# A four-layer graph network on one core: a new instruction plan for the pair distances, statistics by group, and layer 0 of the first groups ahead of the branch

## The chip, the core and the metric

The kernel runs on one core of a Trainium2 chip. A core has five engines that work through their own queues of instructions side by side: TensorE (PE, matrix products into PSUM), VectorE (DVE), ScalarE (ACT), GpSimd (POOL) and SyncE (SP, which here only issues transfers). They hand work to each other by semaphores; transfers between the large memory and the on-chip memory run on DMA engines. The metric is the time of one execution on the device in microseconds (us), from the first to the last instruction; the lower the better. Before the change it is 2890.65 us, the median of three runs (2886.53 to 2890.78).

## What is computed

128 graphs of 128 nodes with 128 features each (`x`), and their adjacency (`adj`, here zeros and ones), go through four residual layers. What matters here is cut from the reference:

```python
# layer 0
h = relu(layernorm(x))
for r in 1..7:                       # one relation per value of adj
    mask = (adj == r); degree = clip(mask.sum(axis=2), 1e-6)
    agg += (mask / degree @ h) @ rel_weights[r]
x = x + relu(layernorm(agg + h @ self_w.T + self_b) * gamma + beta)

# layer 1: attention from pairwise distances
h = relu(layernorm(x))
D = abs(h[:, :, None, :] - h[:, None, :, :])      # [128, 128, 128, 128]
p = D @ W1.T + b1                                 # 64 channels for each pair of nodes
p = (p - mean(p)) / sqrt(var(p) + eps) * g1 + be1 # statistics over all pairs of all graphs
A = softmax(where(adj > 0, leaky(p) @ W2.T + b2, -9e15))
y = A @ h @ Wg.T + bg;  y = leaky(batchnorm(y))   # statistics over all graphs
x = x + concat(h, y) @ Wt.T + bt
# layers 2 and 3: graph attention with 4 heads and with 1, each with its residual
```

Layer 1 needs the mean and the variance of `p` over all pairs of all graphs before any pair can be normalised. So the kernel has three stages: the first computes `p` for all graphs and writes it out, the second reads it back, and the third does layers 2 and 3.

## The kernel before

The graphs are handled in 32 groups of four (`G = 4`, `NG = 32`, `NB = 128`). A distance is symmetric, so only half of the pairs are computed, in four tiles per graph (`NT = 4`). Each tile passes through four engines:

```python
def difference(i):        # "d": tiles 0 and 2 on DVE, 1 and 3 on POOL
    eng = nc.gpsimd if on_pool else nc.vector
    eng.tensor_tensor(d, ahead, x[:, None, None, :].to_broadcast([P, 2, KC, P]),
                      OP.max if t == BY_MAX else OP.subtract)
def absolute(i):          # "abs": ACT; not for tile 0, which goes by the maximum
    nc.scalar.activation(diffs[i], diffs[i], AF.Abs)
def products(i):          # "hp": PE, 8 products for a tile, 16 for tile 0
    ... nc.tensor.matmul(hp[64 * hh:64 * hh + 64, c:c + 512], w1T2 if by_max else w1T, d[:, hh, c:c + 512], ...)
def evacuate(i):          # "hs": ACT copies PSUM out
    nc.scalar.copy(halves[b][:, t, :], linear.pop(i))
def statistics(i):        # "st": DVE
    nc.vector.bn_stats(st[:, 2 * t, :], hs[:, 0:512])
    nc.vector.bn_stats(st[:, 2 * t + 1, :], hs[:, 512:1024 - P * last])
    if last:
        nc.vector.bn_stats(st[:, 8, :], hs[:, 1024 - P:])
        nc.vector.bn_aggr(ST1[:, b, 0, :], st.rearrange("p a b -> p (a b)"))
        nc.vector.bn_aggr(ST1[:, b, 1, :], st[:, 8, :])
```

Beside the tiles, each group has the chain of layer 0 (`chain(g)`: load, two norms, degree, transposes, products, sum, and the norm `h1` that the distances start from) and two steps `features`, which transpose two graphs (`xp`), copy them (`xe`), double a part of the copy on POOL (`again`) and form a small product (`pw`, `xw`).

The order of instructions in the first stage isn't found by hand. Every step is declared with its engine, an assumed duration, the steps that it follows and a rank; a planner builds one list from them, engine by engine in time, and the kernel is emitted in that order. `HOP` is the assumed delay when work passes from one engine to another:

```python
PERIOD, FIRST, HOP, LANDING = 12.5, 4, 0.2, 3.0
def _ordered(steps, limits):
    def released(name):
        engine = named[name][1]
        ready[engine][name] = max([0.0] + [done[a] + HOP * (named[a][1] != engine) for a in waits[name]])
    ...     # the engine that can start first takes its ready step of lowest rank
...
step(("hs", i), "ACT", 0.9, [("hp", i), ("hs", i - 1)] + ..., i + 1, lambda: evacuate(i))
step(("st", i), "DVE", 1.8 if t == NT - 1 else 1.2, [("hs", i), ("st", i - 1)], i + 2, lambda: statistics(i))
```

Ahead of the first stage stands a prologue. The largest value in `adj` decides a branch: only if it is above 1 must relations 2 to 7 be computed. The whole of `adj` (8.4 MB) is scanned for it. In the order of the program: the inputs of the first two groups (`AHEAD = 2`) are asked for, `adj` is scanned in eight parts of 1 MB on DVE (four issued from ACT, four from SP, four buffers), layer 0 of the two groups runs up to its product, then the set-up for layers 2 and 3, then the branch, and behind it the rest of layer 0 of these groups:

```python
for c in range(8):
    part = sc.tile([P, n], I32, name="part", bufs=4)
    (nc.scalar if c < 4 else nc.sync).dma_start(part, flat[c])
    nc.vector.tensor_reduce(tops[:, c:c + 1], part, AX.X, OP.max)
...
for w in first:
    while next(w) != "rest":     # layer 0 of groups 0 and 1, up to the sum
        pass
nc.vector.tensor_scalar(flag, top, 1.5, None, op0=OP.is_gt)
...     # set-up for layers 2 and 3: transposes, small products, bounds, pieces in bf16
with tc.If(nc.values_load(flag, min_val=0, max_val=1) > 0) as cmp: ...   # relations 2 to 7
with cmp.Else():
    ...   # the sum starts from self_b
for _ in itertools.zip_longest(*first):
    pass                         # the rest of layer 0 of groups 0 and 1
```

Of the kernel before, what the change touches and what calls it, by code (L numbers as in the profile page):

```python
# [18 lines left out]
G = 4  # L19
# [13 lines left out]
AHEAD = 2  # L33
FETCHED = 10
# [5 lines left out]
PERIOD, FIRST, HOP, LANDING = 12.5, 4, 0.2, 3.0  # L40
TINY = 2.0 ** -100
# [71 lines left out]
def _ordered(steps, limits):  # L113
# [13 lines left out]
    def released(name):  # L127
        engine = named[name][1]
        ready[engine][name] = max([0.0] + [done[a] + HOP * (named[a][1] != engine) for a in waits[name]])
# [5 lines left out]
    while len(plan) < len(steps):  # L135
# [20 lines left out]
        for tag in gives:  # L156
            left[tag].append(start + cost + HOP)
# [9 lines left out]
def tile_gnn_stack(ctx: ExitStack, tc: tile.TileContext, a: dict, out: bass.AP):  # L167
# [47 lines left out]
    ST1 = res.tile([P, NB, 2, 2], F32, name="ST1")  # L215
# [41 lines left out]
    with tc.tile_pool(name="c0", bufs=1) as c0, tc.tile_pool(name="p0", bufs=2) as p0:  # L257

        both = c0.tile([P, 2, P], F32, name="both")
        nc.sync.dma_start(both[:, 0, :], a["rel_w"][1])  # L260
        nc.sync.dma_start(both[:, 1, :], a["self_wT"])
# [6 lines left out]

        AGG = [c0.tile([P, G, P], F32, name=f"agg{g}") for g in range(AHEAD)] + AGG
# [5 lines left out]

        def highest(sc):

            n = NB * P // 8
            tops = sc.tile([P, 8], F32, name="tops")
            flat = a["adj"].rearrange("b t s -> b (t s)").rearrange("b (c n) -> c b n", c=8)  # L280
            for c in range(8):
                part = sc.tile([P, n], I32, name="part", bufs=4)
                (nc.scalar if c < 4 else nc.sync).dma_start(part, flat[c])
                nc.vector.tensor_reduce(tops[:, c:c + 1], part, AX.X, OP.max)
            top = sc.tile([P, 1], F32, name="top")
            nc.vector.tensor_reduce(top, tops, AX.X, OP.max)
            pt = sm("ptop")
            nc.tensor.transpose(pt[0:1, 0, :], top, ident)
            nc.vector.tensor_reduce(top[0:1, :], pt[0:1, 0, :], AX.X, OP.max)
            return top[0:1, :]  # L290
# [8 lines left out]
        def act_norm(dst, src, rs, nb):  # L299

            for k in range(G):
                nc.scalar.activation(dst[:, k, :], src[:, k, :], AF.Relu, bias=nb[:, k:k + 1],
                                     scale=rs[:, k:k + 1])
# [4 lines left out]

        def layer0(g):
            bs = slice(g * G, g * G + G)  # L310
            x = p0.tile([P, G, P], F32, name="x")
            nc.sync.dma_start(x, a["x"][bs].rearrange("b t c -> t b c"))
            adj = p0.tile([P, G, P], I32, name="adj")
            nc.sync.dma_start(adj, a["adj"][bs].rearrange("b t s -> t b s"))
            yield
            mv = small.tile([P, G, 2], F32, name="lnmv")
            rs = small.tile([P, G], F32, name="lnrs")
            norm_stats(x, mv, rs)
            nb = shift(mv, rs)
            yield  # L320

            mask = p0.tile([P, G, P], F32, name="mask")
            nc.gpsimd.tensor_scalar(mask, adj, 1, None, op0=OP.is_equal)
            deg = small.tile([P, G], F32, name="deg")
            nc.vector.tensor_reduce(deg, mask, AX.X, OP.add)
            nc.vector.tensor_scalar(deg, deg, 1e-6, None, op0=OP.max)
            nc.vector.reciprocal(deg, deg)
            yield
            h = p0.tile([P, G, P], F32, name="hn")
            act_norm(h, x, rs, nb)  # L330
            nc.gpsimd.tensor_tensor(mask, mask, deg[:, :, None].to_broadcast([P, G, P]), OP.mult)
            nc.gpsimd.tensor_scalar(M8[g], adj, 0, None, op0=OP.is_gt)
            yield
            hT = p0.tile([P, G, P], F32, name="hT")
            transpose(hT, h)
            yield
            maskT = p0.tile([P, G, P], F32, name="maskT")
            transpose(maskT, mask)
            yield
            o = p0.tile([P, G, P], F32, name="o")  # L340
            hw = p0.tile([P, G, P], F32, name="hw")
            ph = sm("ph")
            for k in range(G):
                nc.tensor.matmul(ph[:, k, :], hT[:, k, :], both[:, 0, :], start=True, stop=True)
            nc.scalar.copy(hw, ph)
            yield
            po = sm("po")
            for k in range(G):
                nc.tensor.matmul(po[:, k, :], hT[:, k, :], both[:, 1, :], start=True, stop=False)
                nc.tensor.matmul(po[:, k, :], maskT[:, k, :], hw[:, k, :], start=False, stop=True)  # L350
            nc.vector.tensor_copy(o, po)
            yield "rest"
            nc.vector.tensor_tensor(o, o, AGG[g], OP.add)
            yield
            mv = small.tile([P, G, 2], F32, name="lnmv")
            rs = small.tile([P, G], F32, name="lnrs")
            norm_stats(o, mv, rs)
            yield
            for k in range(G):
                nc.vector.scalar_tensor_tensor(o[:, k, :], o[:, k, :], mv[:, k, 0:1], gamma,  # L360
                                               op0=OP.subtract, op1=OP.mult)
            yield
            on = sm("on")
            for k in range(G):
                nc.vector.scalar_tensor_tensor(on[:, k, :], o[:, k, :], rs[:, k:k + 1], beta,
                                               op0=OP.mult, op1=OP.add)
            nc.vector.scalar_tensor_tensor(x, on, 0.0, x, op0=OP.max, op1=OP.add)
            nc.sync.dma_start(X[g], x)
            yield
            norm_stats(x, MV1[:, g], RS1[:, g])  # L370
            nb = shift(MV1[:, g], RS1[:, g])
            yield
            H1[g] = p0.tile([P, G, P], F32, name="h1", bufs=3)
            act_norm(H1[g], x, RS1[:, g], nb)


        H1 = {}
        first = [layer0(g) for g in range(AHEAD)]
        for w in first:
            next(w)  # L380
        with tc.tile_pool(name="sc", bufs=1) as sc:
            top = highest(sc)
            flag = const.tile([1, 1], I32, name="flag")
            for t, v in ((gamma, "gamma"), (beta, "beta")):
                nc.vector.tensor_copy(t, load(v, [P, P], _bcast(a[v], P), pool=c0))
            for k in range(G):
                nc.sync.dma_start(selfb[:, k, :], _bcast(a["self_b"], P))
            for w in first:
                while next(w) != "rest":
                    pass  # L390
            nc.vector.tensor_scalar(flag, top, 1.5, None, op0=OP.is_gt)

        with tc.tile_pool(name="sw", bufs=1) as sw:


            w2x = const.tile([P, P + 8], F32, name="w2x")
            nc.sync.dma_start(w2x[:, 0:P], a["W_2"])
            w3x = const.tile([P, P + 2], F32, name="w3x")
            nc.sync.dma_start(w3x[:, 0:P], a["W_3"])
            b_2 = load("b_2", [P, P], _bcast(a["b_2"], P))  # L400
            b_2c = col("b_2c", a["b_2"])
            wtyT = load("wtyT", [P, P], a["WtT"][P:2 * P])
            a2 = const.tile([P, 2, 4], F32, name="a2")
            nc.vector.memset(a2, 0.0)
            a3 = const.tile([P, 2, 1], F32, name="a3")
            for part in range(2):
                for hd in range(4):

                    nc.sync.dma_start(a2[32 * hd:32 * hd + 32, part, hd:hd + 1], a["a_2"][32 * (1 - part):][0:32])
                nc.sync.dma_start(a3[:, part, :], a["a_3"][P * (1 - part):][0:P])  # L410
            add_b = sw.tile([P, 8], F32, name="add_b")
            bounds = sw.tile([P, 3, 8], F32, name="bounds")
            nc.vector.memset(bounds, 0.0)
            square = sw.tile([P, 10], F32, name="square")
            for wx, av, n in ((w2x, a2, 4), (w3x, a3, 1)):
                pt = sm("pwt")
                nc.tensor.transpose(pt[:, 0, :], wx[:, 0:P], ident)
                wt = sw.tile([P, P], F32, name=f"wt{n}")
                nc.scalar.copy(wt, pt[:, 0, :])
# [23 lines left out]
            nc.vector.tensor_copy(b_parts, part)  # L443
            ones3 = const.tile([3, P], BF16, name="ones3")
            nc.vector.memset(ones3, 1.0)
            nc.vector.tensor_tensor(bounds[:, 2, :], add_b, add_b, OP.mult)


            bound = sw.tile([P, 1], F32, name="bound")
# [1120 lines left out]
```

## Time and profile before

| | |
|---|---|
| time, median of three runs | 2890.65 us |
| span of the profiled execution | 2889.8 us, mean granted PE clock 0.952 |
| busy: PE, DVE, ACT, POOL | 2469.7, 2520.0, 2392.2, 1729.1 us |
| first distance on DVE starts | 81.24 us |
| first stage: first and last rows of `p` issued to memory | 102.98 and 1597.75 us |
| second stage: first and last rows read back | 1604.1 and 2346.5 us |
| last statistic of the second stage | 2410.51 us |

A line of a timeline gives start and duration in us, engine, source line, operation, `out<-in` by the program's names with shapes, how many instructions are merged, and in brackets how long the engine was idle before them and what released it. A line of busy time by stretch gives the stretch, its length, the busy time of PE, of PE's weight loads, of DVE, ACT and POOL with the number of instructions, then the granted PE clock (1.00 is full speed), the DMA engines' share and GB/s. Where the four engines are nearly equally busy, the share alone doesn't tell which of them sets the pace; the period of a repeated instruction and the waits do.

### The profile page before, as it was taken

To read this page: it belongs to the slowest core of one execution; us is meant where nothing else is said; L and a number is where in the kernel's file an instruction comes from. 1 tells how busy PE (TensorE), PEld (TensorE's weight loads), DVE (VectorE), ACT (ScalarE), POOL (GpSimd) and SP (SyncE) were. 2 spreads that over 40 slices of the span, in tenths; PEclk is the share of its full clock that TensorE was granted. 3 is DMA by queue.
4 is the path that set the end of the run, shared out by engine and by line. 5 is a ranking of instruction groups with operands and counts; after the bars stand their busy time and mean duration, and the time that the engine had idled before them with its cause. 6 is when DMAs were issued, how large, how long until landed. Compare 5 with 4: busy or idle time off the path is not lost.

```text
span 2889.8 us, 41921 instructions
## 1 busy us (share of the span) xinstructions
PE 2469.7 (85%) x14517; PEld 1185.7 (41%) x14517; DVE 2520.0 (87%) x4949; ACT 2392.2 (83%) x2811; POOL 1729.1 (60%) x1613
## 2 busy tenths in 40 slices
PE   1899899999898989898989688888888886998897
PEld 1333333333333333333333234444444444777675
DVE  5799999999999999999999578888888885987886
ACT  1799998989899999999999678777877774988886
POOL 2899989898989899898988001101111104665552
PEclk8899999999999999999999899999999997999998
DMA  5555545454544444454544999999999971111210
GB/s 200 201 202 221 204 190 204 190 204 190 204 193 200 195 199 200 193 207 186 215 171 204 368 408 408 410 409 409 410 410 410 408 283 54 45 59 63 63 34 27
DMA packets 180083, 653.83 MB, mean 226 GB/s; under 512 B 30992, under 2 KB 99472, under 8 KB 129680
## 3 DMA queue, kind: packets, MB, share of 16 engines
q1 hardware_dynamic: 179280, 646.80, 56.3%
q10 hardware_dynamic: 576, 4.19, 0.4%
q8 instruction: 119, 1.95, 0.3%
q14 instruction: 108, 0.88, 0.1%
HBM read 338.14 MB, written 312.80 MB: 225 GB/s over the span
## 4 chain that ended last, share of the span: by engine, by line
PE 36%; ACT 23%; DMA 20%; DVE 12%; issue 5%; POOL 3%; SPq 0%; DVEq 0%; ACTq 0%; POOLq 0%
PE hp L595 17%; ACT d L624 11%; DMA z<-hp 7%; DMA rows<-sk 7%; PE hp L598 5%; ACT hs L608 5%; DMA u<-rows 5%; DVE d L585 3%; PE pv L1292 2%; ACT o L717 2%; PE ps L919 1%; ACT h L1176 1%; DVE z L962 1%; PE po L741 1%; POOL rs L221 1%
## 5 line engine op out<-in xcount | busy, mean ns | idle before, releaser
L585 POOL TENSOR_TENSOR d<-xe 128x2048 f32<-128x2048 f32 x256 | 1074.0, 4201 | 86.2 <-PE hp L595 65.7
L595 PE MATMUL hp<-d,w1T 128*64 128x512 f32 x4096 | 1019.2, 621 | 123.1 <-ACT d L624 65.4
L624 ACT ACTIVATE d<-d 128x2048 f32<-128x2048 f32 x384 | 730.9, 1922 | 9.2 <-POOL d L585 5.0
L585 DVE TENSOR_TENSOR d<-xe,xp 128x2048 f32<-128x2048 f32 x256 | 579.9, 2265 | 28.6 <-PE xp L660 21.2
L608 ACT COPY hs<-hp 128x1024 f32<-128x1024 f32 x512 | 512.1, 1017 | 80.2 <-PE hp L598 43.3
L595 PEld LDWEIGHTS hp<-d,w1T 128*64 128x64 f32 x4096 | 290.9, 142 | 691.7 <-issue 465.3
L1008 POOL TENSOR_TENSOR x<-x,bt 128x512 f32<-128x512 f32 x32 | 43.7, 1366 | 684.7 <-DMA x<-x 684.7
L615 DVE BATCH_NORM_STATS2 st<-hs 128x6 f32<-128x512 f32 x512 | 348.8, 681 | 51.6 <-ACT hs L608 51.6
L616 DVE BATCH_NORM_STATS2 st<-hs 128x6 f32<-128x512 f32 (+1 forms) x512 | 328.7, 642 | 0.0
L962 DVE SCALAR_TENSOR_TENSOR z<-z 128x2048 f32<-128x2048 f32 x128 | 297.0, 2320 | 22.8 <-ACT z L944 22.8
L944 ACT ACTIVATE z<-z,bias,scale 128x2048 f32<-128x2048 f32 x128 | 267.3, 2088 | 18.8 <-DMA z<-hp 18.8
L948 ACT ACTIVATE zr<-z,bias,scale 128x2048 f32<-128x2048 f32 x128 | 267.4, 2089 | 9.7 <-DMA z<-hp 7.5
L598 PE MATMUL hp<-both_t,xw 128*64 128x512 f32 x1024 | 266.2, 594 | 0.0
L919 PE MATMUL ps<-z,w2z 128*32 128x512 f32 x1024 | 141.7, 626 | 83.2 <-DVE z L962 83.2
L926 PEld LDWEIGHTS pk<-pick,su 128*128 128x128 f32 x1024 | 125.7, 193 | 139.9 <-DVE su L940 103.0
L926 PE MATMUL pk<-pick,su 128*128 128x16 f32 x1024 | 138.2, 267 | 25.8 <-DVE su L940 24.7
L1292 PE MATMUL pv<-wr,e 128*128 128x128 f32 x1024 | 148.4, 293 | 10.7 <-DVE e L1269 6.1
L1292 PEld LDWEIGHTS pv<-wr,e 128*128 128x128 f32 x1024 | 133.8, 204 | 19.7 <-issue 3.8
L919 PE MATMUL ps<-z,w2l 128*32 128x512 f32 x1024 | 139.1, 612 | 0.6 <-DMA z<-hp 0.6
L919 PE MATMUL ps<-zr,w2r 128*32 128x512 f32 x1024 | 139.0, 615 | 0.4 <-ACT zr L948 0.4
L598 PEld LDWEIGHTS hp<-both_t,xw 128*64 128x64 f32 x1024 | 78.1, 138 | 143.1 <-issue 142.5
L1269 DVE SCALAR_TENSOR_TENSOR e<-e,ps 128x512 f32<-128x512 f32 x160 | 106.8, 678 | 28.7 <-ACT ps L1266 27.9
(266 smaller groups left out, 3855.5 us busy)
## 6 DMA issues: line engine op xcount, KB each, us to landing
hp<-hs SPq DMA_DIRECT2D x128, 2048.0 KB, 6.3
z<-hp SPq DMA_DIRECT2D x256, 1024.0 KB, 14.8
x<-x SPq DMA_DIRECT2D x128, 256.0 KB, 4.8
u<-rows SPq DMA_DIRECT2D x32, 384.0 KB, 11.6
x<-in_x_dram SPq DMA_DIRECT2D x32, 256.0 KB, 3.0
adj<-in_adj_dram SPq DMA_DIRECT2D x32, 256.0 KB, 3.4
out_dram<-x SPq DMA_DIRECT2D x32, 256.0 KB, 2.5
agg<-a SPq DMA_DIRECT2D x30, 256.0 KB, 3.8
```

What stands on the lines that cost most here:

```text
L585: eng.tensor_tensor(d, ahead, x[:, None, None, :].to_broadcast([P, 2, KC, P]), OP.max if t == BY_MAX else OP.subtract)
L595: nc.tensor.matmul(hp[64 * hh:64 * hh + 64, c:c + 512], w1T2 if by_max else w1T, d[:, hh, c:c + 512], start=True, stop=not by_max, skip_gr ...
L598: nc.tensor.matmul(hp[64 * hh:64 * hh + 64, c:c + 512], XW[i // NT // 2][:, i // NT % 2, :], both_t.rearrange("p h k i -> p h (k i)")[:, h ...
L608: nc.scalar.copy(halves[b][:, t, :], linear.pop(i))
L615: nc.vector.bn_stats(st[:, 2 * t, :], hs[:, 0:512])
L616: nc.vector.bn_stats(st[:, 2 * t + 1, :], hs[:, 512:1024 - P * last])
L624: nc.scalar.activation(diffs[i], diffs[i], AF.Abs)
L919: nc.tensor.matmul(ps[32 * c:32 * c + 32, :], w[:, w0:w0 + 32], v[:, 512 * c:512 * c + 512], start=j0 == 0, stop=w is w2r, skip_group_chec ...
L944: nc.scalar.activation(z0, z0, AF.Identity, bias=bias1, scale=scale1[:, 0:1])
L948: nc.scalar.activation(zr, z1, AF.Relu, bias=bias1, scale=scale1[:, 0:1])
L962: nc.vector.scalar_tensor_tensor(z0, z0, 0.01, z0, op0=OP.mult, op1=OP.max)
L1292: nc.tensor.matmul(t[pv][:, k % 2, hd, :], t[e][:, hd, :], flat[:, at:at + P], start=True, stop=True)
```

## The change

It has four parts.

The plan: the assumed durations are replaced by measured ones, and the hop between engines in the first stage's plan is 0.4 us instead of 0.2. The load of the partial sums `agg` becomes a step of its own.

The statistics: the aggregation of the tiles' statistics is done once for a group of four graphs instead of once for each.

The prologue: layer 0 of groups 0 and 1 is declared as steps of the same planner, together with the scan, and is done whole ahead of the branch. The scan has sixteen parts of 0.5 MB, all issued from SP, reduced on DVE and ACT in turn (ACT by a sum of `relu(adj - 1)`). The vectors that all partitions need are spread by a product with ones instead of by transfers. Weights that are used later are loaded later.

The set-up for layers 2 and 3 moves to the end of the second stage.

The diff, cut to its core:

```diff
+PARTS = 16
+HOP1 = 0.4
-def _ordered(steps, limits):
+def _ordered(steps, limits, hop):
-        ready[engine][name] = max([0.0] + [done[a] + HOP * (named[a][1] != engine) for a in waits[name]])
+        ready[engine][name] = max([0.0] + [done[a] + hop * (named[a][1] != engine) for a in waits[name]])
...
-    ST1 = res.tile([P, NB, 2, 2], F32, name="ST1")
+    ST1 = res.tile([P, NG, 2, 2], F32, name="ST1")
...  statistics(i)
-                nc.vector.bn_stats(st[:, 8, :], hs[:, 1024 - P:])
-                nc.vector.bn_aggr(ST1[:, b, 0, :], st.rearrange("p a b -> p (a b)"))
-                nc.vector.bn_aggr(ST1[:, b, 1, :], st[:, 8, :])
+                nc.vector.bn_stats(st[:, 2 * NT, :], hs[:, 1024 - P:])
+            if last and b % G == G - 1:
+                of_all = stats.pop(b // G).rearrange("p a g b -> p a (g b)")
+                nc.vector.bn_aggr(ST1[:, b // G, 0, :], of_all[:, 0:2 * NT, :].rearrange("p a b -> p (a b)"))
+                nc.vector.bn_aggr(ST1[:, b // G, 1, :], of_all[:, 2 * NT, :])
...  durations in the plan
-            engine, cost, rank = ("Pool", 4.25, i - 3) if t in ON_POOL else ("DVE", 2.2, i - 2)
+            engine, cost, rank = ("Pool", 4.22, i - 3) if t in ON_POOL else ("DVE", 2.2, i - 2)
-            step(("st", i), "DVE", 1.8 if t == NT - 1 else 1.2, ...
+            step(("st", i), "DVE", (1.3 if b % G < G - 1 else 2.4) if t == NT - 1 else 1.21, ...
-            step(("rs", g), "Pool", 1.8, ...        # also rso, rsx
+            step(("rs", g), "Pool", 1.95, ...
-            step(("hn", g), "ACT", 1.2, ...         # also oc; h1: 0.6 to 0.78
+            step(("hn", g), "ACT", 1.55, ...
-            step(("xw", n), "ACT", 0.27, ...        # xe: 0.33 to 0.3; hT, maskT, hw: 0.52 to 0.5
+            step(("xw", n), "ACT", 0.18, ...
...  prologue
-        for c in range(8): ...                      # the scan, layer0(g) as generators
+        for c in range(PARTS):
+            step(("part", c), "SP", 20.0 / PARTS, [("top", c - PARTS // 2)], 1 + c / PARTS, lambda c=c: part(c))
+            step(("top", c), "ACT" if c % 2 else "DVE", 1.25, [("part", c)], -99, lambda c=c: highest(c))
+        ...
+        for g in range(AHEAD):
+            chain(g, selfb)
+        with tc.manual_schedule():
+            for work in _ordered(steps, {"sm": 2}, HOP1):
+                work()
         with tc.If(nc.values_load(flag, min_val=0, max_val=1) > 0) as cmp, ...
...
-            for t in AGG[:AHEAD]:
-                nc.vector.tensor_copy(t, selfb)
-        for _ in itertools.zip_longest(*first):
-            pass
...  the set-up for layers 2 and 3, before ahead of the branch
+        def brief():
+            ...
+            at(end, "a", scratch);  at(end, "p", transposed);  at(end + 1, "am", copied)
+            at(end + 1, "p", products);  at(end + 2, "l", squares);  at(end + 3, "p", sums)
+            at(end + 4, "l", compared);  at(end + 1, "l", joined)
+            for n in range(3):
+                at(end + 5 + n, "l", lambda n=n: piece(n))
+            at(end + 8, "l", owners)          # end = NB + 1, in slots of the second stage
```

## The prediction

> **What bounds the kernel now.** I read the page first (busy shares and the 40 slices), then cut the span into stages with the busy time by stretch, then went into one group of the first stage with the timeline of each engine, and last read the prologue's timeline and the chain of work. The slices show four engines working near full from the third slice to the 22nd, each slice being 72 us:
>
> ```profile
> DVE  5799999999999999999999578888888885987886
> ACT  1799998989899999999999678777877774988886
> POOL 2899989898989899898988001101111104665552
> PEclk8899999999999999999999899999999997999998
> ```
>
> The first stage (pair distances of 32 groups of four batches) therefore runs from about 81 us, the first distance on DVE, to 1598 us, the last copy out of PSUM. The rows of HP leave once per batch, the first issued at 102.98 us and the 128th at 1597.75 us: 1494.8 us for 31.75 groups, 47.08 us a group. No other engine has DVE's load. One group's worth of time, 46.4 us, taken early in the stage:
>
> ```profile
> 271.00:317.40 46.40, 41.75 (x206) 16.11 (x204) 45.07 (x84) 43.66 (x48) 43.19 (x27) 1.00 0.50 204
> ```
>
> The columns are PE, weight loads, DVE, ACT, POOL, then the granted clock: DVE works 45.1 of 46.4 us. So DVE is the floor, and the others are within 1.4 to 3.4 us of it. But the rest of the stage is slower than this. The POOL copy that doubles a pair of batches' features comes at the same place in every group; its starts give the period:
>
> ```profile
> 262.95 0.30 POOL L669 COPY xe<-xe 128x128 f32<-128x128 f32 x1
> ...
> 309.33 0.28 POOL L669 COPY xe<-xe 128x128 f32<-128x128 f32 x1
> ...
> 1313.45 0.30 POOL L669 COPY xe<-xe 128x128 f32<-128x128 f32 x1
> ...
> 1361.24 0.30 POOL L669 COPY xe<-xe 128x128 f32<-128x128 f32 x1
> ```
>
> 46.38 us early, 47.79 us later, with the same instructions. The mean clock falls from 1.00 to 0.96 between the two. In a group at 486 us it is seen why. ACT's order is copy, copy, absolute value; the second copy must wait for PE's tile, and the absolute value that PE needs next stands behind it:
>
> ```profile
> 486.47 1.01 ACT L608 COPY hs<-hp 128x1024 f32<-128x1024 f32 x1 [0.39 <-PE hp L598]
> 488.19 1.01 ACT L608 COPY hs<-hp 128x1024 f32<-128x1024 f32 x1 [0.70 <-PE hp L595]
> 489.10 3.71 ACT L624 ACTIVATE d<-d 128x2048 f32<-128x2048 f32 x2
> ```
>
> ```profile
> 491.06 5.35 PE L595 MATMUL hp<-d,w1T 128*64 128x512 f32 x16 [2.32 <-ACT d L624]
> ```
>
> ```profile
> 492.00:494.00 2.00, 2.00 (x8) 0.56 (x6) 2.00 (x3) 2.00 (x4) 2.00 (x1) 0.50 0.00 0
> ```
>
> PE stands still for 2.32 us, and then runs sixteen matmuls in 5.35 us instead of 3.6 (a run of sixteen at 514.25 us) at half clock.
>
> The prologue takes 81 us before the first distance. Three lines of its timeline carry the reading: the flag, the first work behind the branch, the first distance:
>
> ```profile
> 41.45 0.14 DVE L391 TENSOR_SCALAR flag<-top 1x1 int32<-1x1 f32 x1
> ...
> 63.14 0.76 DVE L557 COPY agg<-selfb 128x512 f32<-128x512 f32 x2 [1.36 <-SPq L512]
> ...
> 81.24 2.29 DVE L585 TENSOR_TENSOR d<-xe,xp 128x2048 f32<-128x2048 f32 x1 [6.25 <-PE xp L660]
> ```
>
> Up to 41 us the scan of adj holds everything (DVE waits 6.76 us for one part at 24.27 us). From 41 to 63 us the set-up for layers 2 and 3 and the product of layer 0 run one after the other. From 63 to 81 us the rest of layer 0 runs, a chain of small work with only two groups.
>
> **What the Trainium skill says.** "TensorE: Matmul & The Clock Gate", Part 1: the PE clock is halved after an idle window of about 3.4 us, the windows run freely (3413 ns each), and a busy window brings it back. The trace agrees in rate and length: clock 0.50, and from the shares of the 2 us stretches (0.81 in 490 to 492, 0.83 in 494 to 496) the dip lasts from 491.24 to 494.66 us, 3.42 us. It goes further than the page: a gap of 2.3 us was enough. Fourteen windows are 47.78 us, and the late period is 47.79; I read this as the loop having locked onto the windows, each group's gap falling into the same phase. The same page (its paragraph on queue depths) says ACT and DVE are strictly first in, first out; the ACT lines above are that. "Trainium Kernel Development and Optimization", Key Constraints: queues of all engines share the same 16 DMA engines. So issuing the scan from SP alone loses nothing; in the trace, the first group's x, issued behind four 1 MB parts from ACT, landed 8 us late.
>
> **The change, part by part.**
>
> (A) Prologue. The scan is 8.4 MB, the first two groups' inputs 1 MB. The stretch from 20 to 40 us moved 323 GB/s: 9.4 / 0.323 = 29 us, plus about 2 us to start, so the scan lands near 31 us. Its sixteen reductions are half the size (2.28 / 2 = 1.15 us) and shared by DVE and ACT; maximum, transpose and flag take 1 us more: flag near 33 us. Now the whole of layer 0 runs beside it. From the rows of before, one group's chain is: three statistics of 1.2, three roots of 1.7, three ACT norms of 1.65, two transposes with copies 2.4, product and copy 1.65, second product 1.8, four DVE operations of about 0.68: 13.65 + 2.4 + 1.65 + 1.8 + 2.7 = 22 us, and some 17 handoffs of 0.1 us. With x landing near 5 us and a second group and the scans in the same queues I take 34 us for both: 39 us, so this chain ends last, not the scan. Then the branch (2.9 us in the chain of before, at 60.19) and from transposes to the first distance about 3 us: first distance near 45 us instead of 81. Gain 36 us.
>
> (B) The plan. The order of instructions changes: where ACT had "copy of tile 4n, copy of 4n+1, absolute value of 4n+2", it now has "copy of 4n, absolute values of 4n+2 and 4n+3, copy of 4n+1". PE's 1.7 us of tile 4n+1 now lies beside the 0.9 + 1.9 us of ACT, which leaves about 1.1 us of idle, not 2.3. I expect the dips, and with them the lock, to go. That alone is 47.8 to 46.4 in most groups. With longer hops in the plan, the two DVE waits of the late groups (0.8 us each for a copy by ACT) and one for PE (0.6) should partly go.
>
> (C) Statistics. Before: two aggregations per batch. In line they cost 0.36 us (1016.77 to 1017.13 us), 1.44 a group. After: one of 216 - 24 = 192 numbers and one of 24, once per group. The kernel has a 192-number one already:
>
> ```profile
> 2411.24 1.02 DVE L1083 BATCH_NORM_AGGREGATE mv<-ST 128x2 f32<-128x192 f32 x1
> ```
>
> With the small one about 1.05 in line: 0.4 us saved per group on the bounding engine.
>
> DVE's floor is then 45.1 - 0.4 = 44.7 us. Before, the undisturbed groups left 1.3 us above the floor; I allow 0.9: 45.6 us. (47.08 - 45.6) x 31.75 = 47 us.
>
> (D) The set-up of layers 2 and 3 moves to the end of the second stage. It is some 30 short DVE operations (about 6 us), six small PE products, three ACT copies. DVE is busy 5.61 of 10 us in 2390 to 2400, and 2.78 in the next 10, so most is hidden; I charge 2 us. The second stage itself is bound by transfers (DMA digit 9, 410 GB/s) and doesn't change.
>
> Sum: 2890.65 - 36 - 47 + 2 = 2809.65, say 2810.
>
> **The rivals.** First, the lock stays: PE still idles long enough, somewhere, to lose its clock, and a group is again pulled to 14 windows, 47.8 us. For it: the trace shows how little is needed, and 45.6 is under 47.8. Against it: the one gap above 2 us is gone by the order. It would leave only the prologue: about 2855 to 2865. Second, the plan is worse: with longer hops the planner spreads work, and POOL or ACT (43.2 and 43.7 of 46.4) get a wait instead; a period of 46.4 without dips gives 2835. Third, a gain at the floor: 44.8 us a group and a prologue done at 42 us, 2781. Fourth, in the prologue the chain doesn't run beside the scan, because a DVE or ACT reduction waits for its part ahead of a step of the chain; the gain falls to 25 us.
>
> **Range and chances.** Between floor and plan without dips lie 2781 and 2835; a late prologue adds 10. The lock I give about one in six, which widens the top: 2780 to 2852. The 2% line is 2832.8; all cases without dips and with a period up to 46.2 lie below it. Faster by over 2%: 0.77, within 2%: 0.22, slower: 0.01.
>
> **What would show it.** A: the first distance in the timeline at 41 to 50 us. B: the period of the POOL copy at 45 to 46.2, the clock at 1.00 in the stretches of the stage, no wait of PE for ACT above 2 us. C: 32 aggregations of 128x192 with 1 us each, DVE over 97% busy in the stage. D: less than 4 us more from the last fetch to the third stage. A period of 47.8 with a clock of 0.96 would make the prediction wrong.

## The result and the profile after

The changed kernel takes 2813.82 us (median of four runs, 2811.84 to 2817.27) against 2889.04 us before: a ratio of 0.9742, 95% interval 0.9725 to 0.9758. The profiled execution spans 2811.9 us, mean granted PE clock 0.961.

These are the 40 slices of the changed kernel (one slice is 70 us):

```profile
PEclk7999999999999999999998899999999997999998
DVE  4899999999999999999997588888888886988786
ACT  4899999999999999999997787788888755988886
POOL 6799999999999999999985000111000115655552
```

In the second slice DVE and ACT show an 8 instead of a 7, and the full part ends within the 22nd slice instead of filling it. In this view the change of the clock isn't seen: 0.96 and 1.00 are both a 9. The POOL copy that gave the period before gives it again here:

```profile
1205.95 0.29 POOL L395 COPY xe<-xe 128x128 f32<-128x128 f32 x1
...
1224.81 0.29 POOL L395 COPY xe<-xe 128x128 f32<-128x128 f32 x1
...
1251.56 0.30 POOL L395 COPY xe<-xe 128x128 f32<-128x128 f32 x1
```

There are two copies a group; from the first to the third it is 45.61 us (47.79 before). The late part of the stage by stretch, before and then after, says where that comes from:

```profile
500.00:1300.00 800.00, 723.20 (x3428) 278.41 (x3428) 755.93 (x1378) 734.70 (x787) 723.91 (x436) 0.97 0.49 199
```

```profile
500.00:1300.00 800.00, 745.50 (x3578) 289.01 (x3576) 775.44 (x1329) 760.17 (x822) 758.73 (x455) 1.00 0.52 208
```

The clock is 1.00, and DVE, the bounding engine, is busy 96.9% of the stretch instead of 94.5%. PE's longest wait in this stretch was 2.3 us for the absolute value; now it is 0.9 us for a copy:

```profile
PE hp L595 <- ACT d L624: 37.2, 16, 2.3
```

```profile
PE hp L319 <- ACT hs L333: 44.2, 88, 0.9
```

(Columns: us waited in total, times, longest.) Before 500 us the stage isn't so clean. Two gaps of PE, one of 2.28 us (the line below) and one of 1.95 us at 299.03 us, each brought slow products once (the clock is 0.97 from 200 to 250 us and from 300 to 350 us), but no lock followed:

```profile
234.94 5.35 PE L319 MATMUL hp<-d,w1T 128*64 128x512 f32 x16 [2.28 <-ACT d L350]
```

The statistics show what the change wrote; the columns behind the bar are busy us in total and mean ns:

```profile
L346 DVE BATCH_NORM_AGGREGATE ST<-st 128x2 f32<-128x192 f32 x32 | 32.1, 1004 | 0.0
L347 DVE BATCH_NORM_AGGREGATE ST<-st 128x2 f32<-128x24 f32 x32 | 6.6, 205 | 0.0
```

Before, the two forms had 51.1 and 15.8 us: 66.9 - 38.7 = 28.2 us less by the records. The prediction priced it at 0.4 us a group in line; it is twice that. From the start of a graph's last statistic to DVE's next work it was 0.67 us (1016.46 to 1017.13 us) in each of four graphs before; now it is 0.19 us in three of them and 1.24 us (1218.15 to 1219.39 us) in the fourth: 2.68 - 1.81 = 0.87 us a group.

One figure looks wrong at first. The timeline of DVE in the prologue:

```profile
33.00 0.14 DVE L580 TENSOR_SCALAR flag<-top 1x1 int32<-1x1 f32 x1
...
49.30 4.49 DVE L309 TENSOR_TENSOR d<-xe,xp 128x2048 f32<-128x2048 f32 x2 [0.41 <-ACT xw L390]
74.35 0.87 DVE L427 BATCH_NORM_STATS2 lnst<-x 128x6 f32<-128x128 f32 x4 [20.56 <-DMA x<-in_x_dram]
```

The first distance starts 31.9 us earlier than before. But after two distances DVE waits 20.56 us for the `x` of a later group. The chain of work names what that transfer stood behind:

```profile
47.07 22.60 DMA a<-selfb
...
71.51 2.81 DMA x<-in_x_dram
```

`a<-selfb` is the fill behind the branch: it writes `self_b` into the partial sums of the other 30 groups, 7.9 MB. Before, it ran too, but while DVE still had prologue work; now the stage is there before it is done.

So the landmarks moved like this (rows of HP are the rows of `p` written out):

| landmark | before, us | after, us | gained so far |
|---|---|---|---|
| flag | 41.45 | 33.00 | 8.5 |
| first distance on DVE | 81.24 | 49.30 | 31.9 |
| last rows of HP issued | 1597.75 | 1526.3 | 71.5 |
| first, last rows read back | 1604.1, 2346.5 | 1532.8, 2269.2 | 71.3, 77.3 |
| last aggregation of the second stage | 2411.24 | 2337.07 | 74.2 |
| end | 2889.8 | 2811.9 | 77.9 |

### The profile page after: what moved, and what is told of

Its sections match the earlier page's. It is cut to its first block, busy times and chain, and to the rows that moved or that the text cites. A ratio compares the mean times of both kernels' runs of the same rounds, so it can differ in the third digit from the quotient of the medians.

```text
span 2811.9 us, 41767 instructions
## 1 busy us (share of the span) xinstructions
PE 2466.4 (88%) x14521; PEld 1190.8 (42%) x14521; DVE 2472.0 (88%) x4713; ACT 2392.2 (85%) x2837; POOL 1723.5 (61%) x1628
## 4 chain that ended last, share of the span: by engine, by line
ACT 34%; PE 25%; DVE 21%; DMA 7%; issue 7%; POOL 5%; SPq 0%; ACTq 0%; DVEq 0%; POOLq 0%
ACT d L350 14%; ACT hs L333 10%; PE hp L319 6%; PE ps L849 6%; DVE z L892 4%; DVE d L309 3%; PE hp L322 2%; PE pv L1319 2%; DMA z<-hp 2%; POOL d L309 2%; PE pk L856 2%; DMA rows<-sk 2%; ACT o L450 1%; ACT h L491 1%; ACT hn L450 1%
## 5 line engine op out<-in xcount | busy, mean ns | idle before, releaser
L319 PE MATMUL hp<-d,w1T 128*64 128x512 f32 x4096 | 997.5, 602 | 120.3 <-ACT hs L333 84.4
L856 PE MATMUL pk<-pick,su 128*128 128x16 f32 x1024 | 140.5, 269 | 15.8 <-DVE su L870 15.8
```

The source lines that it names most:

```text
L856: nc.tensor.matmul(pk[:, kk, 0:16], su[:, kk, :], pick.rearrange("p h j -> p (h j)"), start=True, stop=True)
```

## The experiments

The ratio is to the kernel before on the same chip. The kernel before took 2884.9 to 2889.7 us on the chips of these runs, so the difference of two times from different chips can be off by some 5 us. "Last HP" is when the last rows of `p` are issued (1597.75 us before, 1526.3 after); "period" is that of a group in the steady part; the clock is that of the stretch from 500 to 1300 us.

| kernel | time, us | ratio, 95% interval | last HP, us | period, us | clock |
|---|---|---|---|---|---|
| late_constants | 2809.40 | 0.972 (0.9703 to 0.9736) | 1523.4 | 45.6 | 1.00 |
| early_inputs | 2794.64 | 0.9678 (0.9661 to 0.9694) | 1506.7 | 45.63 | 1.00 |
| hop_02 | 2837.70 | 0.9818 (0.9801 to 0.9834) | 1550.8 | 46.68 | 1.00 |
| filled_gap | 2858.14 | 0.9892 (0.9876 to 0.9909) | 1569.2 | 46.49 | 1.00 |
| plan_only | 2859.19 | 0.9896 (0.9879 to 0.9913) | 1572.6 | 45.67 and 47.36 | 0.97 |
| agg_by_batch | 2831.24 | 0.9799 (0.9782 to 0.9816) | 1539.1 | 46.07 | 1.00 |
| old_durations | 2827.04 | 0.9788 (0.9771 to 0.9805) | 1537.5 | 46.33 | 1.00 |
| early_hop_06 | 2775.80 | 0.9614 (0.9593 to 0.9635) | 1486.3 | 44.75 | 1.00 |
| plan_and_stats | 2825.10 | 0.9792 (0.9776 to 0.9809) | 1543.1 | 45.66 | 1.00 |
| stats_numbers | 2868.69 | 0.9941 (0.9924 to 0.9957) | 1577.5 | 47.03 | 1.00 |
| early_hop_08 | 2796.49 | 0.9696 (0.968 to 0.9712) | 1509.1 | irregular | 0.99 |
| early_late_06 | 2781.60 | 0.9639 (0.9623 to 0.9655) | 1494.7 | 44.75 | 1.00 |

### What holds the prologue: late_constants and early_inputs

Two things stood in SP's queue ahead of group 3's `x`: the fill, and small loads of constants. late_constants takes the small loads out of the way (they are 30; the expectation counts 33), early_inputs the dependence on the fill.

```diff
 # late_constants
-b1 = col("b1", a["b1"], 64)    ... 30 loads, ahead of the plan
 for n, work in enumerate(_ordered(steps, {"sm": 2}, HOP1)):
     work()
+    if n == 1000:
+        b1 = col("b1", a["b1"], 64)    ... the same 30 loads
```

> The changed kernel, with its 33 small loads of later weights put behind the 1000th step of the first stage's plan, instead of ahead of the first step. The load of group 3's inputs then comes right behind the fill of the partial sums (7.9 MB) in SP's queue. In the changed kernel DVE waits 20.56 us for that load. Theory Q (queue): the small loads ahead of it hold SP, as each waits for an earlier transfer in its turn; without them the load is issued at 48 us, lands at 52, and about 20 us are won: 2794 us. Theory R (rings): the load's packets stand behind the fill's in the DMA engines, so an early issue lands late all the same, near 70 us; less than 5 us are won: 2809 to 2814 us.

The SP timeline and then the DVE timeline of late_constants:

```profile
44.10 1.34 SPq L677 DMA_DIRECT2D a<-selfb  x2
45.98 12.93 SPq L417 DMA_DIRECT2D x<-in_x_dram  x1
```

```profile
68.54 0.87 DVE L428 BATCH_NORM_STATS2 lnst<-x 128x6 f32<-128x128 f32 x4 [16.81 <-DMA x<-in_x_dram]
```

`x` is now the next transfer behind the fill, issued 25.5 us earlier than in the changed kernel, and lands 5.8 us earlier. The time falls by 4.4 us, as theory R had it: the small loads cost those few microseconds, and the fill holds the rest.

```diff
 # early_inputs
-nc.sync.dma_start(tile0("x"), ...)           # adj alike
+nc.sync.dma_start(tile0("x", bufs=3), ...)
-step(("load", g), "SP", 1.2, [...]
+step(("load", g), "SP", 1.2, [...] * (g != AHEAD + 1)     # group 3 waits for no buffer
-chain(AHEAD)                        # the load of group 2 goes ahead of the branch
+for g in (AHEAD, AHEAD + 1):        # those of groups 2 and 3 do
+    chain(g) ...
```

> The changed kernel with the inputs of group 3 loaded ahead of the branch, so ahead of the fill (three buffers for x and adj instead of two); the small loads stay where they are. Under both Q and R the wait of DVE at 54 us goes and about 20 us are won: 2794 us. If SP, held by the small loads until 70 us, makes the first rows of p wait instead (their issue later than 75 us), a part is given back: 2800 us. If nothing is won, the wait at 54 us wasn't on the path.

The SP timeline and then the DVE timeline of early_inputs:

```profile
21.94 0.43 SPq L416 DMA_DIRECT2D x<-in_x_dram  x1
...
41.80 0.39 SPq L416 DMA_DIRECT2D x<-in_x_dram  x1
```

```profile
46.66 0.87 DVE L427 BATCH_NORM_STATS2 lnst<-x 128x6 f32<-128x128 f32 x4 [7.16 <-DMA x<-in_x_dram]
...
49.57 4.47 DVE L309 TENSOR_TENSOR d<-xe,xp 128x2048 f32<-128x2048 f32 x2
56.63 2.29 DVE L309 TENSOR_TENSOR d<-xe,xp 128x2048 f32<-128x2048 f32 x1 [2.58 <-PE hp L319]
```

The wait of 20.56 us is gone; the third distance starts at 56.63 instead of 75.41 us. The last rows of HP come 19.6 us earlier with the same period, and the time falls by 19.2 us. The page "DMA: Bandwidth & Descriptors" of the Trainium skill, section "Queues, rings and completion order", says that the transfers of SP share one row of rings and that each DMA engine consumes its descriptors in ring order. The trace agrees: in late_constants group 3's `x`, issued at 45.98 us behind the fill, landed only at 68.5 us, when the 22.7 us of the fill were over. In early_inputs it was issued at 21.94 us, ahead of the branch, and DVE doesn't wait for it at all; the 7.16 us before 46.66 us are for the `x` of group 2, issued at 41.80 us.

### How much of the gain is the clock: filled_gap

The kernel before, with six products added where PE stood still; their results are overwritten by the products that follow.

```diff
 by_max = i % NT == BY_MAX
+if i % (G * NT) == 10:
+    for c, hh in ((0, 0), (0, 1), (512, 0), (512, 1), (0, 0), (0, 1)):
+        nc.tensor.matmul(hp[64 * hh:64 * hh + 64, c:c + 512], w1T, both_t[...], start=True, stop=True)
```

> The kernel before, with six extra products of 512 columns on PE (1.3 us) ahead of the products of the one tile of each group for which PE waits 2.3 us; they write the same PSUM tile, which the real products then overwrite. Order, waits and data are otherwise those of before. Theory L (the wait costs more than itself, because PE's clock falls to a half and the loop locks to the windows): the dips go, the clock rises from 0.96 to 1.00 in the first stage, the period falls from 47.8 to 46.4 us in the late groups: 30 to 40 us faster than before, 2850 to 2860 us, although work is added. Rival W (the period is set by DVE and the waits alone, the dip is hidden): no gain, 2887 to 2893 us.

```profile
500.00:1300.00 800.00, 759.64 (x3720) 294.18 (x3722) 775.77 (x1409) 750.70 (x810) 742.61 (x447) 1.00 0.50 203
```

PE does more, and the kernel is 30.7 us faster than the kernel before in the same runs: the clock is 1.00, the period 46.49 in all late groups. The stage shrinks from 1494.8 to 1465.9 us. So 28.8 us of the old stage came from PE at half clock, after one gap a group; filling the gap without any change of order shows it.

### Plan and statistics apart: plan_only, stats_numbers, plan_and_stats, agg_by_batch

plan_only puts the hop of 0.4 and changed durations into the kernel before. More exactly than its expectation says: ten of the changed durations (POOL's distance, the statistics' 1.21, `xe`, `xw`, `rs`, `hn`, `hT`, `maskT`, `hw`, `o`); `rso`, `rsx`, `oc` and `h1` kept their old ones, and the load of `agg` stayed in its old step. The same holds for the next two kernels.

```diff
 # plan_only, on the kernel before
+HOP1 = 0.4          # and HOP1 for HOP in _ordered
-("Pool", 4.25, i - 3) ... "Pool", 1.8, own("mv") ... "ACT", 1.2, own("rs") ... "ACT", 0.27, [("pw"
+("Pool", 4.22, i - 3) ... "Pool", 1.95, own("mv") ... "ACT", 1.55, own("rs") ... "ACT", 0.18, [("pw"
```

> The kernel before with the changed one's durations and hop of 0.4 in its plan, nothing else: its prologue and its aggregation per batch stay. Theory B (the plan carries the stage's gain, through the clock and shorter waits; the statistics give only the 0.4 us of DVE per group): HP rows from 103 us on, stage 1494.8 - 54.2 + 12.7 = 1453, period near 46.0, clock 1.00, time near 2848 us. Rival C (the statistics by group carry much of it, because the two aggregations per batch sit at the place in the order where ACT and PE wait): period 46.5 or more, time 2858 or more, like the kernel before with its gap filled.

The time is the rival's, but not for its reason: the dips are still there. The POOL copies of plan_only, each second one of a group:

```profile
538.00 0.29 POOL L670 COPY xe<-xe 128x128 f32<-128x128 f32 x1
...
583.67 0.29 POOL L670 COPY xe<-xe 128x128 f32<-128x128 f32 x1
...
631.02 0.30 POOL L670 COPY xe<-xe 128x128 f32<-128x128 f32 x1
...
678.39 0.29 POOL L670 COPY xe<-xe 128x128 f32<-128x128 f32 x1
```

45.67, 47.35, 47.37 us; then 47.37 and again 45.66. PE in the third of these groups, its clock there, and ACT in the same place:

```profile
668.75 5.35 PE L596 MATMUL hp<-d,w1T 128*64 128x512 f32 x16 [2.29 <-ACT d L625]
```

```profile
670.00:672.00 2.00, 2.00 (x6) 0.49 (x4) 2.00 (x5) 2.00 (x5) 2.00 (x2) 0.50 0.00 0
```

```profile
662.95 1.02 ACT L609 COPY hs<-hp 128x1024 f32<-128x1024 f32 x1 [0.39 <-PE hp L599]
663.86 0.61 ACT L731 ACTIVATE hT<-pt 128x512 f32<-128x512 f32 x1
664.98 3.71 ACT L625 ACTIVATE d<-d 128x2048 f32<-128x2048 f32 x2 [0.52 <-POOL d L586]
```

A gap of 2.29 us again, with another cause. The copy of tile 4n+1 has moved behind the absolute values, as predicted. But a copy of layer 0 stands ahead of them, and the first of the two waits 0.52 us for POOL, which makes the distances of tiles 1 and 3; so it is that of tile 4n+3. PE needs tile 4n+2 first and starts at 668.75 us, when both are done (664.98 + 3.71 = 668.69). Three groups in four lose 47.36 - 45.67 = 1.69 us, half of a 3.41 us window at half clock, and the fourth escapes. Four groups take 187.76 us (538.00 to 725.76), which is 55 windows of 3.414 us: I read this as the loop locked onto the windows again, at another ratio.

stats_numbers changes only numbers of the plan: the instructions stay those of plan_only.

```diff
-step(("st", i), "DVE", 1.8 if t == NT - 1 else 1.21, ...
+step(("st", i), "DVE", (1.3 if b % G < G - 1 else 2.4) if t == NT - 1 else 1.21, ...
```

> The run with the plan alone (2859.2 us), but with the plan told 1.3, 1.3, 1.3 and 2.4 us for the last statistics of the four batches, where it was told 1.8 for each; the instructions themselves stay two aggregations per batch. Theory G1 (the order that follows from these numbers takes the gap away): clock 1.00, period 46.0 to 46.2, 2843 to 2852 us. Rival G2 (the DVE time itself is needed): gap and dips stay, 2855 to 2862 us.

Both were off. PE's waits of stats_numbers in the stretch from 500 to 1300 us:

```profile
PE hp L596 <- ACT hs L609: 52.2, 67, 1.8
PE hp L596 <- ACT d L625: 20.3, 17, 1.2
```

The gap is 1.8 us at most, the clock is 1.00, as G1 said; yet the period is 47.03 us, above the mean of plan_only (46.94). I read this so: the order is laid out for statistics that take less than these do, and the period pays the difference.

plan_and_stats adds the aggregation by group to stats_numbers, as in the change; its prologue and everything else are those of before.

```diff
-ST1 = res.tile([P, NB, 2, 2], F32, name="ST1")      # and one pair of bn_aggr per graph
+ST1 = res.tile([P, NG, 2, 2], F32, name="ST1")      # and one pair per group
```

> The kernel before with the changed one's durations, hop and statistics by group, but its own prologue. The run with the plan alone kept a gap of 2.3 us (PE waits for the absolute value) and a period of 46.9. Theory G (the group statistics, with their numbers in the plan, bring the gap under 2 us): clock 1.00, period 45.6, stage near 1440 us, last HP row near 1543 us, time 2832 to 2840 us; the changed kernel's prologue is then worth 17 to 22 us. Rival H (it is the changed prologue and chain that moved the order of the stage): gap and dips stay, only 0.4 us per group come: 2843 to 2850 us.

Its waits of PE in the same stretch:

```profile
PE hp L596 <- ACT hs L610: 32.1, 70, 0.9
PE hp L596 <- ACT d L627: 20.3, 17, 1.2
```

Theory G holds: no gap above 1.2 us, clock 1.00, period 45.66 (the time is 7 us below its range, on a chip where the kernel before is 4 us faster too). The numbers alone had removed the dips, at the price of the period; the aggregation brings the period to 45.66, which the groups of plan_only without a dip already had (45.67). The stage is now within 1.5 us of that of the changed kernel (1442.0 and 1440.6), so the difference in the last rows of HP, 1543.1 - 1526.3 = 16.8 us, is what the prologue is worth.

agg_by_batch goes the other way: the changed kernel with two aggregations per graph again (54 and 6 numbers), the plan's numbers untouched.

> The changed kernel with two aggregations per batch again (54 and 6 numbers), the plan's numbers as in the changed kernel. Theory B: DVE does 0.4 us more per group and the period grows by just that, 45.63 to 46.0: plus 9 to 13 us, 2823 to 2827 us. Rival C: the period grows to 46.4 or more, 2838 us or more. Rival N (DVE's spare 3% takes it up): 2814 to 2817 us.

The period is 46.07 instead of 45.63 us. That is B's number, but not quite its reason: DVE does 0.87 us more a group, and half of it went into DVE's spare time. The stage takes 1453.8 us instead of 1440.6. The time grows by 17.4 us, more than B's 9 to 13 and less than C's 24: 13.2 in the stage, and 3.9 in the read-back of the second stage (740.4 instead of 736.5; see the end). The same instructions cost 0.44 us a group here and 47.03 - 45.66 = 1.37 us in the order of stats_numbers.

### The plan's numbers: hop_02, old_durations, early_hop_06, early_hop_08, early_late_06

All five change constants of the plan in the changed kernel; the last three include early_inputs.

```diff
-HOP1 = 0.4
+HOP1 = 0.2      # hop_02; 0.6 in early_hop_06 and early_late_06, 0.8 in early_hop_08
```

> The changed kernel with the hop of the first stage's plan at 0.2 us as before; measured durations, aggregation and prologue stay. Theory H (the hop moves the copy of tile 4n+1 behind the absolute values): PE's gap of over 2 us comes back, the clock dips once in each group, the period is pulled to 47.8 us from 45.6: 55 to 70 us slower, 2870 to 2885 us. Theory D (the measured durations do it): period stays 45.5 to 46.2, clock 1.00, within 15 us of the changed kernel.

No dip, but a wait that the changed kernel hasn't:

```profile
PE pt L460 <- POOL mask L454: 20.6, 17, 1.2
```

The period is 46.68. So neither theory as written: the lock didn't return, and the hop is worth 1.05 us a group. old_durations sets the ten durations listed above back in the changed kernel (the statistics keep 1.3 and 2.4):

> The changed kernel with the durations of the kernel before in its plan, but the hop at 0.4. The run with the hop at 0.2 had no gap and no dip with the new durations. Theory E (either of the two is enough to get ACT's order right): no dips, clock 1.00, period 45.6 to 46.2, 2812 to 2832 us. Rival F (the durations do it, and the hop only trims): ACT's second copy stands before the absolute value again, PE waits over 2 us in a group, clock 0.96 in late stretches, period 46.5 to 47.8, 2842 to 2882 us.

Clock 1.00, but 46.33 us, a little above E's range for the period; 13.2 us slower. Neither the old hop alone nor the old durations alone bring the gap back here; each costs some of the period. Both together, with the statistics' 1.3 and 2.4 kept, weren't tried.

> The version with group 3's inputs ahead of the branch (2794.6 us) and the hop at 0.6 instead of 0.4. From 0.2 to 0.4 the period went from 46.68 to 45.63. Theory T (the real handoffs are longer than 0.4, the trend goes on): period 45.2 or less, 2775 to 2784 us. Theory U (0.4 is near the best, DVE is 97% busy): period 45.5 to 45.8, 2790 to 2800 us. Theory V (too long a hop makes the plan keep too little in flight): 2805 us or more.

T's ranges hold; its reason, real handoffs longer than 0.4 us, wasn't tested. The stretch of early_hop_06:

```profile
500.00:1300.00 800.00, 750.94 (x3644) 292.12 (x3641) 793.63 (x1360) 776.69 (x844) 771.14 (x463) 1.00 0.55 213
```

DVE is busy 99.2%; the period of 44.75 us is close to the floor that the prediction worked out (44.7; DVE's own busy time is 44.4 us a group). With 2775.80 us this is the fastest version of the study.

> Group 3's inputs ahead of the branch and the hop at 0.8 instead of 0.6 (2775.8 us, period 44.75, DVE 99.2% busy). Theory U (the floor of DVE is reached, nothing is left): period 44.6 to 44.8, 2772 to 2780 us. Theory V (a longer hop holds work back): period 45 or more, 2785 us or more.

V's ranges hold. The period became irregular (15.5 to 29.4 us between copies), with PE waits like these:

```profile
590.53 4.49 PE L319 MATMUL hp<-d,w1T 128*64 128x512 f32 x12 [1.80 <-ACT hs L333]
627.40 2.79 PE L319 MATMUL hp<-d,w1T 128*64 128x512 f32 x12 [1.65 <-ACT hs L333]
717.79 2.79 PE L319 MATMUL hp<-d,w1T 128*64 128x512 f32 x12 [1.99 <-ACT hs L333]
```

Twelve products after 1.80 us run slow, after 1.99 us at full clock: it isn't the length of one gap alone that decides.

> Group 3's inputs ahead of the branch, the small constants behind the 1000th step of the plan, hop 0.6. Theory R (once group 3's inputs are in place, nothing else that the stage waits for stands in the queue): within 4 us of 2775.8. Rival S (the small loads still hold up partial sums or the 4th group's inputs): 2764 to 2770 us.

Neither: it is 5.8 us slower, and its last rows of HP come 8.4 us later. At the start of the stage the loads cost nothing (the first rows of the second group leave at 114.3 us, and at 114.8 us in early_hop_06), as R had it. But the 30 loads, put behind the 1000th step, were still in the way, as POOL's timeline shows:

```profile
455.49 1.50 POOL L438 TENSOR_SCALAR mask<-adj 128x512 f32<-128x512 int32 x1 [10.43 <-DMA adj<-in_adj_dram]
```

SP issued them from 432.9 to 451.7 us, 19 us, and the inputs of a group stood behind them; the interval between two copies there is 38 us instead of 27.5. At hop 0.4 the same place cost less: in late_constants that wait was 5.0 us and the stage 2.8 us longer than in the changed kernel (1443.4 and 1440.6).

## Why the time came out as predicted, step by step

The time is 4 us from the predicted 2810, and that is luck. The prologue brought 19.2 us less than predicted; plan and statistics brought 7.6 us more, and the second and third stages, which were to stay as they were but for the set-up, another 9.6 us.

**(A) Prologue: mechanism right, worth half.** The flag came at 33.00 us (33 predicted); layer 0 of both groups ended 4.6 us late, at 43.6 (39), and so the first distance came at 49.30 (45). The step that failed is the equation "first distance earlier" = "gain": 36 us predicted; the first distance came 31.9 us earlier, and the end of the stage only 16.8, between plan_and_stats and the changed kernel (they ran on different chips, which can be 2 to 3 us of it). I had left out that the fill of the partial sums runs behind the branch and that the next group's inputs queue behind it. early_inputs takes that away and returns 19.6 us at the end of the stage. That 16.8 and 19.6 make the 36 is partly luck: the first distance of early_inputs (49.57 us) is 29.6 us ahead of that of plan_and_stats (79.18), and the other 6.8 us were won in the first rounds of the stage. The rival "chain doesn't run beside the scan" can be behind the 4.6 us at most. One reading was wrong: the first group's `x` didn't land 8 us late before; it took 8 us from its issue (1.67 to 9.6 us), against 3 us in the changed kernel (0.73 to 3.7).

**(B) Plan and (C) statistics: 47 predicted, 54.6 measured** (last rows of HP at 1597.75 and 1543.1 us). The period was met, 45.6 predicted and 45.63 measured, and from 500 us on clock 1.00 and waits below 2 us as well. The sum was low because the stage's ends are shorter than a period: the mean over 31.75 groups is 45.37. The predicted order is there. ACT does the copy of tile 4n, both absolute values, and then the copy of 4n+1:

```profile
1239.37 1.01 ACT L333 COPY hs<-hp 128x1024 f32<-128x1024 f32 x1 [0.93 <-PE hp L322]
1240.28 3.71 ACT L350 ACTIVATE d<-d 128x2048 f32<-128x2048 f32 x2
1243.89 1.00 ACT L333 COPY hs<-hp 128x1024 f32<-128x1024 f32 x1
```

PE, with the rest of tile 4n+1 done, has a product of layer 0 in this place and then starts tile 4n+2, after 0.1 us of idle time (1.1 predicted):

```profile
1240.98 1.16 PE L468 MATMUL ph<-both,hT 128*128 128x128 f32 x8
1242.25 1.94 PE L319 MATMUL hp<-d,w1T 128*64 128x512 f32 x8
```

What I had wrong is the share of the parts. I gave the end of the dips to this move of the copy; plan_only, with most of the new numbers, has it too and keeps a gap of 2.29 us. The kernels differ in this way: in the ten whose plan has 1.3 and 2.4 for the last statistics and a hop up to 0.6, no gap above 1.8 us is left from 500 to 1300 us; in the two that have 1.8 and no filling, before and plan_only, there is one of 2.3. Whether these numbers would do it alone, with the old hop and the old durations, wasn't tried, nor the whole set of durations with 1.8. The price of (C), 0.4 us a group, was half of what DVE saved, 0.87 us; in agg_by_batch 0.44 us of it show in the period. The clock part is separate and shown: 28.8 us by filled_gap.

**DVE over 97% busy:** 96.9% from 500 to 1300 us, so the planner left 3%. early_hop_06 took most of it. The rival "gain at the floor" (2781) was open to the design; it needed a hop of 0.6 and the inputs ahead.

**(D) Set-up moved: 2 predicted, 3.1 measured.** From the last read-back to the last aggregation, five kernels without it take 64.5 to 65.8 us, and the nine with it 66.7 to 68.7.

**Not in the sum:** the second stage's reading is 5.9 us shorter (742.4 to 736.5), and the third stage 3.7 (478.5 to 474.8, which varies by as much among the runs). Then 54.6 + 16.8 + 5.9 + 3.7 - 3.1 = 77.9 us, the whole difference of the spans (3.1 is D in this one pair).

The rival "lock stays" fell for the changed kernel, but plan_only shows that it was near: stats_numbers, which has no dips, differs from it by one duration of the plan.

## What to carry to other kernels

When a prologue gets shorter, price it at the next thing that the steady loop waits for, not at its first instruction, and look at what the same queue has to move before that; here a fill of 7.9 MB ate half of the gain. In a planned loop on four engines near full, fill PE's largest gap before anything else, and tune the planner's hop by measurement: 0.2, 0.4 and 0.6 gave a period of 46.68, 45.63 and 44.75 us (the last with early inputs, which alone left the period at 45.63), and 0.8 broke the rhythm. What a DVE instruction is worth depends on the order around it: the same aggregations were worth 0.44 us a group in one order and 1.37 us in another.

## What the runs showed of the hardware that was not expected

- A PE gap of 2.3 us is enough for half clock, though not in each group. The Trainium skill's "TensorE: Matmul & The Clock Gate", Part 1, speaks of an idle window of about 3.4 us; here a shorter gap did it, and the measurement decides. Gaps of 1.8 us in stats_numbers never did from 500 to 1300 us; one of 1.80 us in early_hop_08 did and one of 1.99 didn't.
- A loop with such a gap settles on whole windows: 47.79 us is 14 of 3.414 us, and plan_only settled on 55 of the same length in four groups (187.76 us).
- All nine kernels with statistics by group read back in the second stage in 733.8 to 737.4 us, and all five with statistics by graph in 739.9 to 742.4. The work between the stages is under 1 us different, the lead grows along the whole stage, and the transfers run at 412 GB/s instead of 409 (1650 to 2250 us, changed kernel and before). The cause stays open.
